# Two more engines in a hand-written order: GpSimd's sums, SyncE's loads and the copy of O^T in a graph-attention kernel

## The chip, the cores and the metric

The kernel runs on one core of a Trainium2 chip. The metric is the device time of one execution in microseconds (us), and lower is better. The kernel before was run three times: 2642.13, 2642.48 and 2645.84 us, so its median is 2642.48 us.

A core has five engines that work side by side, each through its own queue of instructions: TensorE (PE; its weight loads are PEld), VectorE (DVE), ScalarE (ACT), GpSimd (POOL) and SyncE (SP). Here SyncE issues nearly all DMA transfers and computes nothing. An instruction that needs another engine's result waits on a semaphore.

## The reference

There are 128 graphs (blocks) `b` of 128 nodes with 512 features, and a 0/1 adjacency matrix per graph. Two layers follow each other:

```python
# layer 0: attention with 8 heads of 64 features, masked by adj
q, k, v = x @ Wq + bq, x @ Wk + bk, x @ Wv + bv
attn = softmax(where(adj > 0, q k^T / 8, -1e9))        # per head
x = layernorm(x + relu((attn @ v) @ Wo + bo))
# layer 1: graph attention with one head
Wh = x @ W
e = leaky(Wh @ a1 [rows] + Wh @ a2 [columns])          # 128 x 128 per graph
att = softmax(where(adj > 0, e, -9e15), axis=1)        # over the rows
x = layernorm(x + leaky(att @ Wh))
```

## The kernel before

**Products by seven multiplications.** The products with Wq, Wk, Wv, Wo and W are each split into 2 x 2 blocks and done with seven block products in place of eight (`strassen`, a list of seven steps p1, p5, p6, p2, p7, p4, p3). The left operand needs sums of its blocks, which GpSimd makes in `left_blocks` with four additions (L289 to L292): `xS` for x, `oS` for the attention output, `x1S` for the first layer's result. The sums of the weights are made once. Seven weight blocks for Wv [...] lie in DRAM and come back for each group through a ring of three buffers `wv_n` (`fetch`, L402). Each of the seven block products of V first fetches the block that will be wanted two products later.

**Groups, pairs and steps.** Q, K and V are computed for four graphs at a time, a *group*: 3 x 7 = 21 block products (`products`, L361). The products with Wo and W are done for two graphs, a *pair* (`project_o` and `project_w`, both through `pair_product`, L442). One big loop over `t` from -4 to 136 is a software pipeline; one turn is a *step*. In a step, TensorE does the logits of graph `t` (`Softmax`, L486), the attention product of graph `t - 1` (`attend`, L549), five of the group's block products (six where t mod 4 = 3), the seven of a pair (with Wo in odd steps, with W in even steps), and the second layer's small products (`EdgeSoftmax`, `Finish`) for graphs `t - 7` and `t - 8`. The calls `group()` and `pair()` in the loop take the next steps of those lists, so the order of the lines in the loop is a timetable.

**Transposes.** x must be transposed for the products. `load_x` (through `spread`, L257, four DMAs) brings a graph in such a form that VectorE's transpose of 32 x 32 tiles (`transpose_blocks`, L262) completes it. It lands in one of three buffers `xz`. The first layer's result goes the same way: it is normalized (L577), written to DRAM as `x1_dram` (L590), spread back into an `xz` buffer, and transposed into `x1T`. The attention weights `pa` take the same detour: `Softmax.spread` writes `pa_dram` (L528), and when it has landed, reads it as `paz` with four DMAs (L532).

**Normalization.** `norm_stats` takes mean and variance on VectorE and forms `rstd` on GpSimd with two small operations (L571, L573), for which VectorE's `normalize` waits.

**What sets the order.** `tc.manual_schedule(engines=...)` makes the engines that it names keep the order in which the program's lines call them. Before, these are TensorE, VectorE and ScalarE. For GpSimd and SyncE the framework's planner chooses an order by its own costs and priorities, where the data allow it; `norm_stats` asks it for a high priority of the two `rstd` operations. Either way the order is fixed when the kernel is built, and each queue runs in it.

**Around the change.** In the step as written before, a load of x, a residual load (`load_residual`, L273) and a mask load (L465) stand at the start. The last-but-one VectorE lines of a step are `transpose_x(t + 8)`, `mask(t + 1)` and, in even steps, `transpose_x1` for two graphs. The sums `xS` follow the fourth transpose of a group, which lies in the step with t mod 4 = 3. `attend` ends with ScalarE's copy of O^T (L559); in odd steps it begins a new pair and therefore a new use of the only buffer `oT`, which the products with Wo of the pair before read until their last step; in even steps the copy is followed by the sums `oS`. `later` holds work that the next step does right after the logits: the second graph's `store`.

## Time and profile before

| | |
|---|---|
| median of three runs | 2642.48 us |
| the profiled execution's own time | 2641.05 us |
| its span, first to last instruction | 2638.9 us |
| PE busy | 2467.2 us (93%) |
| DVE busy | 1780.2 us (67%) |
| ACT busy | 1355.0 us (51%) |
| POOL busy | 764.3 us (29%) |
| all transfers | 379.89 MB, 144 GB/s |
| mean granted TensorE clock | 0.987 |

The profile is one execution, taken by the hardware profiler. The span is what its records cover; the execution's own time is a little longer. In the timeline, a line gives the start and the duration in us from the span's start, the engine, the line of the kernel, the operation, what it writes and reads, how many instructions were merged, and in brackets how long the engine had been idle before it and what ended that idle time. SPq lines are issues of DMAs, not their transfers; those land later, after the time that the page's table of DMA issues gives. The view of waits lists who waited for whom: the total, how many times, and the longest.

### The profile page before, as it was taken

Reading aid. Unit: us, or ns where it says so; the run is one execution under the profiler, and the core shown is the slowest. Engines: PE = TensorE matmul, PEld = TensorE weight load, DVE = VectorE, ACT = ScalarE, POOL = GpSimd, SP = SyncE. Lnnn points to the kernel's source line nnn. Section 1 sums busy time; section 2 is a strip of 40 time slices with the busy share of each in tenths; the row PEclk is TensorE's granted clock in tenths of the full one; section 3 lists DMA queues with packets and bytes.
Section 4 is the critical chain, followed back from the end, with each engine's and each line's share of the span. In section 5 each row is a group of like instructions: output and inputs, shape, how many; then the busy total and the mean of one; then the engine's idle time right before and its main releaser. Section 6 shows DMA issues by size and latency. Waiting matters only on the chain.

```text
span 2638.9 us, 43141 instructions
## 1 busy us (share of the span) xinstructions
PE 2467.2 (93%) x13717; PEld 1999.8 (76%) x13717; DVE 1780.2 (67%) x3758; ACT 1355.0 (51%) x4801; POOL 764.3 (29%) x1161
## 2 busy tenths in 40 slices
PE   7889999999999999999999999999999999999975
PEld 6767777777777777777777777777777777777753
DVE  4566666676766676766676766676766676766775
ACT  2445455455455555555555555555555555455551
POOL 1122332323332323332323332323332323332222
PEclk9989999999999999999999999999999999999987
DMA  6534454444445444444444445444444444444441
GB/s 186 152 112 133 154 150 148 144 148 143 152 147 153 139 151 143 148 147 156 136 153 143 146 147 156 137 147 144 150 147 155 136 148 144 150 147 152 128 136 49
DMA packets 353348, 379.89 MB, mean 144 GB/s; under 512 B 39640, under 2 KB 257760, under 8 KB 353120
## 3 DMA queue, kind: packets, MB, share of 16 engines
q1 hardware_dynamic: 351824, 376.07, 46.1%
q8 instruction: 109, 1.79, 0.3%
q10 hardware_dynamic: 1296, 1.05, 0.1%
q14 instruction: 119, 0.97, 0.1%
HBM read 240.91 MB, written 136.05 MB: 143 GB/s over the span
## 4 chain that ended last, share of the span: by engine, by line
PE 59%; DVE 15%; ACT 8%; POOL 7%; issue 6%; DMA 3%; SPq 2%; DVEq 0%; ACTq 0%; POOLq 0%
PE st_y L361 14%; PE p_y L442 13%; PE st_w L361 7%; PE st_x L361 6%; PE p_w L442 5%; PE p_oT L549 5%; ACT pa L507 4%; PE lg L486 3%; DVE pa L495 3%; PE p_h L674 2%; PE p_x L442 2%; POOL xS L290 2%; DVE z L683 2%; DVE z L682 2%; DVE xT L262 1%
## 5 line engine op out<-in xcount | busy, mean ns | idle before, releaser
L507 ACT ACTIVATE pa<-pa,nmax 128x128 f32<-128x128 f32 x1024 | 397.7, 391 | 126.6 <-DVE nmax L501 120.5
L521 ACT ACTIVATE pa<-pa,rs 128x128 f32<-128x128 f32 x1024 | 334.3, 397 | 0.6 <-DVE rs L517 0.4
L571 POOL TENSOR_SCALAR ve<-mv 128x1 f32<-128x1 f32 x256 | 62.6, 244 | 934.4 <-DVE mv L568 934.4
L262 DVE STREAM_TRANSPOSE x1T<-xz 128x512 f32<-128x512 f32 x128 | 83.5, 690 | 215.9 <-DMA xz<-x_dram 200.5
L486 PEld LDWEIGHTS lg<-kT,qT 64*128 64x128 f32 x2048 | 124.2, 187 | 93.7 <-issue 93.7
L507 ACT ACTIVATION_READ_ACCUMULATOR pa<-pa,nmax 128x1 f32 x1024 | 193.3, 189 | 0.0
L442 PE MATMUL p_y<-w,x1S 128*128 128x257 f32 x512 | 137.4, 391 | 56.6 <-ACT pr_t L453 56.6
L559 ACT COPY oT<-p_oT 128x512 f32<-128x512 f32 x128 | 74.8, 585 | 214.7 <-PE p_w L442 212.6
L338 ACT COPY st_t<-st_y 128x512 f32<-128x512 f32 x192 | 110.5, 576 | 136.4 <-PE st_y L361 134.0
L453 ACT COPY pr_t<-p_y 128x256 f32<-128x256 f32 (+1 forms) x384 | 139.6, 364 | 77.0 <-PE p_y L442 76.3
L495 DVE TENSOR_TENSOR pa<-lg,mf 128x512 f32<-128x512 f32 x256 | 163.7, 680 | 12.1 <-PE lg L486 8.2
L573 POOL TENSOR_TENSOR rstd<-ve,mhalf 128x1 f32<-128x1 f32 x256 | 166.3, 650 | 18.8
L678 ACT COPY z<-p_h 128x512 f32<-128x512 f32 x128 | 74.9, 585 | 181.7 <-PE p_h L674 181.1
L361 PE MATMUL st_y<-wv_n,xT 128*128 128x256 f32 x512 | 124.4, 386 | 40.9 <-ACT st_t L338 38.5
L536 DVE STREAM_TRANSPOSE paT<-paz 128x1024 f32<-128x1024 f32 x128 | 159.4, 1245 | 4.6 <-DMA paz<-pa_dram 3.9
L342 ACT ACTIVATE st_t<-st_y,b_cols 128x256 f32<-128x256 f32 x192 | 79.8, 467 | 158.3 <-PE st_y L361 158.3
L501 DVE TENSOR_REDUCE nmax<-pa 128x8 f32<-128x1024 f32 x128 | 156.1, 1220 | 4.4
L442 PEld LDWEIGHTS p_y<-w,x1S 128*128 128x128 f32 x512 | 95.3, 192 | 82.3 <-ACT pr_t L453 69.8
L442 PE MATMUL p_y<-wo,oS 128*128 128x256 f32 x512 | 135.9, 388 | 18.1 <-ACT pr_t L453 16.9
L674 PE MATMUL p_h<-wh,att 128*128 128x512 f32 x256 | 133.9, 605 | 18.0 <-DVE att L665 18.0
L289 POOL TENSOR_TENSOR oS<-oT 128x256 f32<-128x256 f32 x64 | 46.5, 726 | 357.0 <-ACT oT L559 357.0
L289 POOL TENSOR_TENSOR xS<-xT 128x512 f32<-128x512 f32 x32 | 40.7, 1273 | 373.0 <-DVE xT L262 357.8
(154 smaller groups left out, 6112.5 us busy)
## 6 DMA issues: line engine op xcount, KB each, us to landing
pa_dram<-pa SPq DMA_DIRECT2D x128, 512.0 KB, 3.0
paz<-pa_dram SPq DMA_DIRECT2D x512, 128.0 KB, 2.9
wv_n<-wv SPq DMA_DIRECT2D x224, 256.0 KB, 2.8
xz<-in_x_dram SPq DMA_DIRECT2D x512, 64.0 KB, 2.2
x<-in_x_dram SPq DMA_DIRECT2D x128, 256.0 KB, 2.8
x_dram<-x SPq DMA_DIRECT2D x128, 256.0 KB, 2.0
xz<-x_dram SPq DMA_DIRECT2D x512, 64.0 KB, 2.2
out_dram<-z SPq DMA_DIRECT2D x128, 256.0 KB, 2.0
```

What stands on the lines that cost most here:

```text
L361: nc.tensor.matmul(p[:, m, :], lhs, rhs, start=start and m == 0 and kc == 0, stop=True, skip_group_check=True,)
L442: nc.tensor.matmul(p[:, :width], xs[n][:, kc, :], w[:, n, kc, :], start=start and kc == 0, stop=True, skip_group_check=True,)
L453: nc.scalar.copy(t[:, :width], p[:, :width])
L486: nc.tensor.matmul(self.lg[r][:, c, :], q[rows, c, cols], k[rows, c, cols], start=True, stop=True)
L495: nc.vector.tensor_add(by_head[:, r * NC : (r + 1) * NC], self.lg[r].rearrange("p c (b k) -> p c b k", b=4), mf.unsqueeze(1).to_broadcast( ...
L501: nc.vector.tensor_reduce(self.nmax, by_head, AX.XY, ALU.max, negate=True)
L507: nc.scalar.activation(self.pa[:, :, h, :], self.pa[:, :, h, :], AF.Exp, bias=self.nmax[:, h : h + 1], accum_out=self.sums[:, h : h + 1],)
L521: nc.scalar.activation(self.pa[:, :, h, :], self.pa[:, :, h, :], AF.Copy, scale=self.rs[:, h : h + 1])
L536: nc.vector.transpose(self.paT.rearrange("p h (a i) -> p a h i", i=32), self.paz.rearrange("p a (h k) -> p a h k", k=32),)
L549: nc.tensor.matmul(p[r * HD : (r + 1) * HD, c, :], v[:, h * HD : (h + 1) * HD], sm.paT[:, r * NC + c, :], start=True, stop=True,)
L573: nc.gpsimd.tensor_tensor(rstd, ve, mhalf, ALU.pow)
L674: nc.tensor.matmul(p.rearrange("p (o f) -> p o f", o=2), edge.att, wh, start=True, stop=True)
```

## The change

SyncE and GpSimd are put under `manual_schedule` too, so that they keep the order of the program's lines. Those lines are moved:

- The transposes of x follow a table `x_turns` by t mod 4: one, two, one and none in place of one per step. The last of a group, and so the sums `xS`, now stands in the step with t mod 4 = 2.
- The loads of x for the next step's transposes stand behind this step's transposes.
- The residual load stands behind `fin.residual()`.
- The first two fetches of Wv's blocks stand at K's first block product instead of its fourth, five block products earlier.
- `attend` returns its copy of O^T (with the sums `oS`) as a function. In even steps it is called at once, in odd steps behind the last two steps of the chain with Wo.
- In `project_o` the first graph's store and the spreads of both graphs are done together at the start of the next step; the second graph's store stays at the end of its chain.
- The exponential of the last head stands behind the output store and one pair product.

```diff
@@ products
-        fetch_first = chains[1][3]
+        fetch_first = chains[1][0]
 ...
-        chains[1][3] = with_fetch
+        chains[1][0] = with_fetch
@@ attend
-        if h == 0:
-            OT[pair] = work.tile([P, NC, 2 * P], F32, name="oT")
-        nc.scalar.copy(OT[pair][:, :, h * P : (h + 1) * P], p)
-        if h == 1:
-            sums = work.tile([P, 3, 2, P], F32, name="oS")
-            OT[pair] = left_blocks(OT[pair], sums)
+
+        def copy():
+            if h == 0:
+                OT[pair] = work.tile([P, NC, 2 * P], F32, name="oT")
+            nc.scalar.copy(OT[pair][:, :, h * P : (h + 1) * P], p)
+            if h == 1:
+                sums = work.tile([P, 3, 2, P], F32, name="oS")
+                OT[pair] = left_blocks(OT[pair], sums)
+
+        return copy
@@ project_o
-        def store(b, stats):
-            normalize(X1[b], stats)
-            d = dram.tile([P, D], F32, name="x1_dram")
-            nc.sync.dma_start(d, X1[b])
-            X[b, 1] = spread(d)
-
-        stats = {}
+        stats, d = {}, {}
+
+        def store(h):
+            b = 2 * pair + h
+            normalize(X1[b], stats[h])
+            d[h] = dram.tile([P, D], F32, name="x1_dram")
+            nc.sync.dma_start(d[h], X1[b])
+
+        def spread_both():
+            store(0)
+            for h in (1, 0):
+                X[2 * pair + h, 1] = spread(d[h])
 ...
-                    store(b + 1, stats[1])
-                    later.append(lambda: store(b, stats[0]))
+                    store(1)
+                    later.append(spread_both)
@@ the loop
-    engines = {mybir.EngineType.PE, mybir.EngineType.DVE, mybir.EngineType.Activation}
+    engines = {
+        mybir.EngineType.PE,
+        mybir.EngineType.DVE,
+        mybir.EngineType.Activation,
+        mybir.EngineType.SP,
+        mybir.EngineType.Pool,
+    }
 ...
+    x_turns = [(8,), (8, 9), (9,), ()]
 ...
-        if on(t + 9):
-            load_x(t + 9)
-        if on(t - 2):
-            load_residual(t - 2)
 ...
         fin.residual()
+        if on(t - 2):
+            load_residual(t - 2)
 ...
-        sm.exp(6, 7)
+        sm.exp(6)
         fin.store()
         pair()
+        sm.exp(7)
 ...
-        if last is not none:
-            attend(last)
+        copy_o = attend(last) if last is not none else none.copy
+        if t % 2 == 0:
+            copy_o()
         sm.spread()
         group()
-        if on(t + 8):
-            transpose_x(t + 8)
+        for b in x_turns[t % GROUP]:
+            if on(t + b):
+                transpose_x(t + b)
+        for b in x_turns[(t + 1) % GROUP]:
+            if on(t + 1 + b):
+                load_x(t + 1 + b)
 ...
         pair(2)
+        if t % 2 == 1:
+            copy_o()
         group(21 if t % GROUP == GROUP - 1 else 1)
```

## The prediction

> **What bounds the kernel now.** Times are in us. I read the page first, then TensorE's waits, then the timeline of one four-step cycle. On the page TensorE is the busy engine:

> ```profile
> span 2638.9 us, 43141 instructions
> ...
> PE 2467.2 (93%) x13717; PEld 1999.8 (76%) x13717; DVE 1780.2 (67%) x3758; ACT 1355.0 (51%) x4801; POOL 764.3 (29%) x1161
> ```

> No other engine is near its limit, so the time moves only with TensorE's idle time, 2638.9 - 2467.2 = 172 us. Its waits (us in total, times, longest) say what is repeated and what happens once:

> ```profile
> PE p_y L442 <- ACT pr_t L453: 75.0, 52, 5.3
> PE st_y L361 <- ACT st_t L338: 38.5, 32, 1.2
> ```

> The first has its long members in the last steps; the second recurs once in each of the 32 groups. Where in the cycle they lie is seen from the starts of the logits (`lg`), the first matmuls of each step:

> ```profile
> 958.78 1.16 PE L486 MATMUL lg<-kT,qT 64*128 64x128 f32 x16
> ...
> 977.08 1.16 PE L486 MATMUL lg<-kT,qT 64*128 64x128 f32 x16
> ...
> 998.79 1.16 PE L486 MATMUL lg<-kT,qT 64*128 64x128 f32 x16
> ...
> 1018.80 1.16 PE L486 MATMUL lg<-kT,qT 64*128 64x128 f32 x16
> ...
> 1037.57 1.16 PE L486 MATMUL lg<-kT,qT 64*128 64x128 f32 x16
> ```

> These start steps with t mod 4 = 2, 3, 0, 1 and again 2. Lengths: 18.30, 21.71, 20.01, 18.77; sum 78.79. Step 2 has no TensorE wait, so 18.30 is the bare length of an even step. An odd step has two bias matmuls more (0.11 + 0.12): 18.53. Step 3 also has a sixth group product (1.73 from its start to the next matmul): 20.26. A cycle without waits is 18.30 + 20.26 + 18.30 + 18.53 = 75.39, so waits cost 3.40: 1.45 in step 3, 1.71 in step 0, 0.24 in step 1. The timeline of step 3 and the beginning of step 0 shows where the first two come from:

> ```profile
> 988.69 0.69 ACT L521 ACTIVATE pa<-pa,rs 128x128 f32<-128x128 f32 x2
> ...
> 989.41 0.32 SPq L528 DMA_DIRECT2D pa_dram<-pa  x1
> ...
> 991.37 0.32 SPq L402 DMA_DIRECT2D wv_n<-wv  x1
> ...
> 993.15 0.58 ACT L559 COPY oT<-p_oT 128x512 f32<-128x512 f32 x1 [3.58 <-PE p_w L442]
> 993.21 2.36 SPq L532 DMA_DIRECT2D paz<-pa_dram  x4
> ...
> 994.28 1.99 PE L361 MATMUL st_y<-wv_n,xT 128*128 128x256 f32 x8 [1.22 <-ACT st_t L338]
> ...
> 995.65 1.27 POOL L289 TENSOR_TENSOR xS<-xT 128x512 f32<-128x512 f32 x1 [10.81 <-DVE xT L262]
> ...
> 996.11 1.89 PE L361 MATMUL st_w<-wv_n,xT 128*128 128x256 f32 x8
> ...
> 1001.79 0.55 DVE L577 TENSOR_SCALAR x<-x,mv,rstd 128x512 f32<-128x512 f32 x1 [2.16 <-POOL rstd L573]
> ```

> ScalarE's copy of O^T holds its queue for 3.58, because the single `oT` buffer is read until the chain with Wo ends. The `st_t` copy behind it is late, and TensorE waits 1.22. VectorE too is set back, and the sums `xS` begin at 995.65, so `rstd` queues behind 5.5 of GpSimd work and VectorE waits 2.16. Its maxima, the exponentials and the `pr_t` copy are late in turn, until the next step's chain shows it:

> ```profile
> 1010.46 1.14 PE L442 MATMUL p_y<-w,x1S 128*128 128x257 f32 x4 [1.44 <-ACT pr_t L453]
> ```

> [...] SP itself waits for `pa_dram` 102 times, 137.4 in all, and nothing passes it. [...] `wv_n` is issued in 0.32 and lands after 2.8. [...] `x<-y,x` (L585) takes 0.69 alone and 1.39 during `xS`.

> **The change part by part.**

> 1. O^T behind the chain. In odd steps the copy comes after the Wo matmuls for which it waited. ScalarE no longer blocks; the 1.45 of step 3 goes. No PSUM bank is held longer, since the copy ended after that chain before.

> 2. Sums in even steps. The last transpose of a group moves from step 3 to step 2, so odd steps have no sums, and both `rstd` of x1 run at once (0.21 + 0.57 after `mv`). VectorE's 2.16 goes. In step 2 GpSimd now runs oS (4 x 0.73), xS (1.27 + 1.26 + 1.72 + 1.26) and x1S (4 x 0.73) in a row: 11.3 from O^T's copy at 13.8 after the step's start, until 25.1, that is 6.8 into step 3, whose z statistics come at 7.5. Hidden, by 0.7; with contention `rstd` may be 1 late, for which ScalarE has 0.7 idle before `pr_t`. Step 1 has two transposes (0.70 more) and VectorE has 1.37 idle there: nothing.

> 3. exp(7) behind `fin.store` and a pair product. ScalarE's pr_t copy is 0.58 (0.39 + 0.19) earlier. With 2, step 0's maxima end near 4 after its start instead of 7.05; the 1.71 goes.

> 4. Loads of x behind the transposes, both x1 spreads after both stores. Before, x1's second spread waited for an x transpose to free one of three `xz` buffers, and VectorE then waited for it (200.5 over the run). Now no load of x holds a buffer that the spreads need. They issue by about 5 into the even step and are needed at 16 or later. The 0.24 of step 1 goes. The x loads, four or eight issues of 0.46, serve the next step's end.

> 5. First two weight fetches (two DMAs) from step 2 to the start of step 1: used in steps 2 and 3, hidden. Mask (one), residual (one, needed about 8 later), and out store keep slack of several us.

> 6. What SP's strict order adds. The seventh weight fetch (`n = 2`) stands in the fourth group product of step 3, directly behind `sm.spread()`. Before, SP issued it at 991.37, ahead of `paz`. Now it comes after: last divide ends 988.69 + 0.69 = 989.38; `pa_dram` issued 989.41; landed 3.0 later (median on the page), 992.4; four `paz` issues, 1.75 (the run of four at 977.19 took 1.77), 994.2; then the fetch, 2.8 if alone, up to 3.3 behind 512 KB of `paz`: 997.0 to 997.5. Its user is the product at 996.11, which without the 1.45 is due at 994.66. TensorE waits 2.3 to 2.8; I take 2.5. Queued behind it are `p_h` and the next logits, so all of it counts. It can't hide earlier: the last divide follows a `pr_t` copy for which the seventh pair product on TensorE is the release. The other fetches stand before the spread.

> Sum per cycle: -3.40 + 2.5 = -0.9; 30 full cycles: -27. In the last steps exp(7) takes some 0.58 off four long waits: -2. The head's four DVE- and DMA-bound steps: 0, between -5 and +5. Against the profiled execution's 2641.05 (span 2638.9, 2.15 around it): 2612; the median shown is 1.4 above that execution: about 2613. Bounds: a fetch wait of 1.8 gives -50, one of 3.3 gives -5.

> **Rivals.**

> A, likeliest: as summed, 2613, own range 2588 to 2637.

> B: the seventh fetch lands in time, because SP can still issue it before `paz`. For it: before, it did. Against it: SP is in the list of ordered engines, and its wait is its own. Time: 2642.5 - 3.40 x 30 - 2 = 2538.

> C, slower: the fetch is later than I think. Place: the same product in step 3. From a wait of 3.40 on, the cycle loses. If `pa_dram` needs 4.0 (from 989.41 it was 3.8 to the first `paz`), `paz` 2.36 as at 993.21, and the fetch 3.3, the data come at 999.1, a wait of 4.4: +1.0 x 30, 2672. Against it: those long figures were made with a weight and a mask transfer among them, which are now elsewhere.

> **How the numbers follow.** A 0.60, B 0.08, C 0.25, and 0.07 that A and C meet near zero. About 0.2% (5.3 us) is what a measurement can tell from no change. Faster is A and B, 0.68; same 0.07; slower 0.25. The range leaves out B and the upper part of C: 2575 to 2670.

> **What would show it.** Right: no 3.58 before the O^T copy, no wait of `x` for `rstd`, x1T not waiting for DMA; steps 0, 1, 2 near 18.3, 18.5, 18.3; step 3 near 22.8 with one wait of 2 to 3 at `st_w<-wv_n,xT` released by DMA `wv_n`. Wrong: that wait absent (B) or over 3.4 (C), or `pr_t` waits left in steps 0 or 1.

## The result, and the profile after

Times are in us. The changed kernel takes 2689.3 (median of 4 runs, 2686.4 to 2692.72) where the kernel before took 2643.95 beside it (4 runs): a ratio of 1.0172, 95% interval 1.0154 to 1.019. It is 1.7% slower; the forecast was 1.1% faster. The profiled execution took 2687.35 with a span of 2685.4, 46.5 more than the span before.

The first part of the page of the changed kernel (busy time of each engine, share of the span, instructions):

```profile
span 2685.4 us, 43419 instructions
PE 2501.6 (93%) x13717; PEld 2033.8 (76%) x13717; DVE 1814.7 (68%) x3758; ACT 1353.9 (50%) x4801; POOL 796.3 (30%) x1161
```

TensorE executes the same 13717 matmuls, and yet it is busy 34.4 longer (2501.6 against 2467.2). A wait counts as idle time, so nearly all of this is matmuls that became longer. Its idle time, 183.8, is only 12 above the 172 of before. TensorE's waits in the changed kernel (us in total, times, longest):

```profile
PE st_w L361 <- DMA wv_n<-wv: 103.6, 31, 4.6
PE p_y L442 <- ACT pr_t L453: 25.9, 13, 5.0
```

The `st_t` wait (38.5) has gone and the `pr_t` wait fell from 75.0 to 25.9. In their place stands one new wait, for the seventh weight fetch, once in each of 31 cycles, 3.34 on average. The starts of the logits in the timeline of one cycle show where it lies:

```profile
1064.37 1.16 PE L486 MATMUL lg<-kT,qT 64*128 64x128 f32 x16
...
1082.68 1.16 PE L486 MATMUL lg<-kT,qT 64*128 64x128 f32 x16
...
1109.33 1.16 PE L486 MATMUL lg<-kT,qT 64*128 64x128 f32 x16
...
1127.63 1.16 PE L486 MATMUL lg<-kT,qT 64*128 64x128 f32 x16
```

Step 2 lasts 18.31, step 3 26.65, step 0 18.30, and step 1 (up to 1146.12) 18.49. Three of four steps have reached their bare length; step 3 alone, against a bare 20.26, spoils the cycle. The timeline of the second half of that step, SP's queue (SPq) and TensorE:

```profile
1094.86 0.70 ACT L521 ACTIVATE pa<-pa,rs 128x128 f32<-128x128 f32 x2
...
1095.58 0.32 SPq L528 DMA_DIRECT2D pa_dram<-pa  x1
...
1098.83 1.79 SPq L532 DMA_DIRECT2D paz<-pa_dram  x4
...
1100.72 0.38 SPq L402 DMA_DIRECT2D wv_n<-wv  x1
...
1103.97 3.75 PE L361 MATMUL st_w<-wv_n,xT 128*128 128x256 f32 x8 [3.59 <-DMA wv_n<-wv]
...
1107.52 1.88 PE L683 MATMUL p_h<-wh,att 128*128 128x512 f32 x2
```

This is the order that part 6 of the prediction described: `pa_dram`, a wait for its landing, four `paz`, then the fetch. But after the wait the eight matmuls of `st_w` take 3.75, where the same eight took 1.89 before, and `p_h` takes 1.88 instead of 1.02. The view of these stretches says why (stretch, its length, PE busy and matmuls, PEld, DVE, ACT, POOL busy, granted TensorE clock, DMA share, GB/s):

```profile
1082.70:1100.40 17.70, 17.68 (x105) 14.84 (x104) 13.50 (x27) 9.61 (x35) 8.48 (x11) 1.00 0.40 129
1100.40:1104.00 3.60, 0.03 (x1) 0.06 (x1) 1.63 (x4) 0.58 (x1) 1.73 (x3) 0.78 0.89 245
1104.00:1107.50 3.50, 3.50 (x8) 2.80 (x9) 0.00 (x0) 0.00 (x0) 0.00 (x0) 0.50 0.31 104
1107.50:1109.30 1.80, 1.80 (x3) 0.34 (x1) 1.15 (x2) 0.00 (x0) 0.00 (x0) 0.52 0.00 0
1109.30:1127.60 18.30, 18.30 (x105) 15.12 (x104) 11.42 (x24) 11.10 (x40) 4.55 (x8) 1.00 0.35 114
```

The granted clock falls from 1.00 to half during the wait, stays there over the next 5.3 us of work, and is full again in the next step. So the wait is paid twice: 3.59 idle, and 5.3 of work at half speed, which loses another 2.8 (26.65 - 20.26 - 3.59). In the whole run the mean clock is 0.966, before it was 0.987.

The step lasts 25.34 on average over 31 cycles: 20.26 bare, 3.34 of wait, and 1.74 that is neither. Without the first cycle, whose bare step is shorter, and against 20.22, the bare length in the runs below, this last loss is 1.86. It isn't spread evenly: 0.24 in 8 cycles, 1.66 to 1.93 in 8, 2.67 to 2.88 in 14. In the 8 cycles the recorded clock stays at 1.00 throughout, so 0.24 comes with the wait itself and 1.62 is the clock's share.

The other thing to see is at the start of step 3. The timeline there, GpSimd (POOL) beside VectorE and ScalarE:

```profile
1086.33 1.23 DVE L691 SCALAR_TENSOR_TENSOR z<-z 128x512 f32<-128x512 f32 x1
...
1087.09 1.05 POOL L290 TENSOR_TENSOR x1S<-x1S,x1T 128x256 f32<-128x256 f32 x1
...
1087.59 1.10 DVE L692 TENSOR_TENSOR z<-z,x 128x512 f32<-128x512 f32 x1
...
1088.62 0.81 DVE L661 SCALAR_TENSOR_TENSOR e<-e 128x128 f32<-128x128 f32 x1
...
1090.18 0.40 ACT L669 ACTIVATE att<-att,nmax 128x128 f32<-128x128 f32 x1 [1.26 <-DVE nmax L665]
```

The same three VectorE instructions in step 3 of the kernel before, where GpSimd's sums had ended at 980.08:

```profile
980.74 0.68 DVE L682 SCALAR_TENSOR_TENSOR z<-z 128x512 f32<-128x512 f32 x1
...
981.45 0.69 DVE L683 TENSOR_TENSOR z<-z,x 128x512 f32<-128x512 f32 x1
...
982.06 0.28 DVE L652 SCALAR_TENSOR_TENSOR e<-e 128x128 f32<-128x128 f32 x1
```

The sums `xS` and `x1S` now end 7.4 into step 3 (6.8 forecast). While they run, VectorE's three instructions take 3.14; before, they took 0.68 + 0.69 + 0.28 = 1.65. ScalarE then waits 1.26 for VectorE (before, it did not wait there), its divides are later, and `pa_dram` is issued 12.91 after the step's start (median), where it was 12.33.

### The profile page after: what moved, and what is told of

The parts are those of the page before. It is cut to its first block, busy times and chain, and to the rows that moved or that the text cites. A ratio compares the mean times of both kernels' runs of the same rounds, so it can differ in the third digit from the quotient of the medians.

```text
span 2685.4 us, 43419 instructions
## 1 busy us (share of the span) xinstructions
PE 2501.6 (93%) x13717; PEld 2033.8 (76%) x13717; DVE 1814.7 (68%) x3758; ACT 1353.9 (50%) x4801; POOL 796.3 (30%) x1161
## 3 DMA queue, kind: packets, MB, share of 16 engines
q8 instruction: 109, 1.79, 0.3%
q10 hardware_dynamic: 1296, 1.05, 0.1%
## 4 chain that ended last, share of the span: by engine, by line
PE 85%; DMA 6%; DVE 4%; ACT 3%; issue 1%; SPq 1%; POOL 0%; DVEq 0%; POOLq 0%; ACTq 0%
PE st_y L361 23%; PE p_y L442 15%; PE st_w L361 14%; PE p_w L442 7%; PE st_x L361 6%; PE lg L486 5%; PE p_h L683 5%; PE p_oT L549 4%; DMA wv_n<-wv 4%; PE p_x L442 4%; DMA pa_dram<-pa 1%; ACT pa L507 1%; ACT pa L521 1%; DVE z L691 1%; DVE z L692 1%
## 5 line engine op out<-in xcount | busy, mean ns | idle before, releaser
L575 POOL TENSOR_SCALAR ve<-mv 128x1 f32<-128x1 f32 x256 | 68.4, 267 | 1362.7 <-DVE mv L572 1362.7
L521 ACT ACTIVATE pa<-pa,rs 128x128 f32<-128x128 f32 x1024 | 332.9, 395 | 0.1
L486 PEld LDWEIGHTS lg<-kT,qT 64*128 64x128 f32 x2048 | 126.3, 190 | 105.9 <-issue 105.9
L338 ACT COPY st_t<-st_y 128x512 f32<-128x512 f32 x192 | 110.2, 574 | 175.9 <-PE st_y L361 175.9
L361 PE MATMUL st_w<-wv_n,xT 128*128 128x256 f32 x256 | 97.3, 547 | 103.6 <-DMA wv_n<-wv 103.6
L379 DVE TENSOR_TENSOR v<-st_w,st_t 128x512 f32<-128x512 f32 x64 | 44.2, 691 | 206.4 <-PE st_w L361 150.1
L577 POOL TENSOR_TENSOR rstd<-ve,mhalf 128x1 f32<-128x1 f32 x256 | 176.0, 688 | 21.3
L453 ACT COPY pr_t<-p_y 128x256 f32<-128x256 f32 (+1 forms) x384 | 140.3, 365 | 77.1 <-PE p_y L442 76.4
L683 PE MATMUL p_h<-wh,att 128*128 128x512 f32 x256 | 148.8, 666 | 18.0 <-DVE att L674 18.0
L289 POOL TENSOR_TENSOR oS<-oT 128x256 f32<-128x256 f32 x64 | 46.3, 724 | 398.1 <-ACT oT L561 398.1
L361 PEld LDWEIGHTS st_w<-wv_n,xT 128*128 128x128 f32 x256 | 67.2, 275 | 127.6 <-issue 106.7
L486 PE MATMUL lg<-kT,qT 64*128 64x128 f32 x2048 | 150.8, 287 | 0.0
L549 PEld LDWEIGHTS p_oT<-paT,v 128*64 128x64 f32 x2048 | 111.2, 138 | 46.0 <-issue 32.9
L442 PE MATMUL p_y<-w,x1S 128*128 128x257 f32 x512 | 133.2, 382 | 13.4 <-ACT pr_t L453 13.4
```

The source lines that it names most:

```text
L361: nc.tensor.matmul(p[:, m, :], lhs, rhs, start=start and m == 0 and kc == 0, stop=True, skip_group_check=True,)
L442: nc.tensor.matmul(p[:, :width], xs[n][:, kc, :], w[:, n, kc, :], start=start and kc == 0, stop=True, skip_group_check=True,)
L453: nc.scalar.copy(t[:, :width], p[:, :width])
L486: nc.tensor.matmul(self.lg[r][:, c, :], q[rows, c, cols], k[rows, c, cols], start=True, stop=True)
L521: nc.scalar.activation(self.pa[:, :, h, :], self.pa[:, :, h, :], AF.Copy, scale=self.rs[:, h : h + 1])
L549: nc.tensor.matmul(p[r * HD : (r + 1) * HD, c, :], v[:, h * HD : (h + 1) * HD], sm.paT[:, r * NC + c, :], start=True, stop=True,)
```

## The experiments

Two theories at first. **F**: the whole loss is the seventh fetch standing behind the spread, by its wait and by the clock that the wait lowers; without it all steps are bare and the kernel is far faster than before. **G**: other parts of the change cost as well (the sums that end late, SP's and GpSimd's strict order), and the fetch only shows it.

**The fetch ahead of the spread.** The changed kernel with the fourth group product, which issues the fetch, one place earlier; nothing else is touched:

```diff
-        sm.spread()
         group()
+        sm.spread()
```

> The changed kernel with one pair of lines exchanged: the fourth group product of a step, with its fetch of a block of Wv, stands ahead of the spread of the attention weights. Theory 1, the late seventh fetch and the clock that falls after the wait for it: both go in all 31 cycles, 31 x (3.34 + 1.74) = 157 us, so about 2532 us, step 3 near 20.3 us, granted clock back at 0.987. Theory 2, GpSimd's three sums in a row in step 2 are what costs: the wait reappears elsewhere in step 3 and the time stays above 2640 us.

Measured: 2528.06 (2 runs), ratio to the kernel before 0.9556 (0.9529 to 0.9584). Its page, and the first line of TensorE's waits, where the fetch is no longer among them:

```profile
span 2525.3 us, 43417 instructions
PE 2446.0 (97%) x13717; PEld 2009.7 (80%) x13717; DVE 1817.4 (72%) x3758; ACT 1355.6 (54%) x4801; POOL 797.1 (32%) x1161
```

```profile
PE p_y L442 <- ACT pr_t L453: 25.3, 11, 5.0
```

The end of its step 3 in the timeline of TensorE, and SP's queue there:

```profile
1024.92 1.89 PE L361 MATMUL st_y<-wv_n,xT 128*128 128x256 f32 x8
1026.64 1.89 PE L361 MATMUL st_w<-wv_n,xT 128*128 128x256 f32 x8
1028.37 1.02 PE L683 MATMUL p_h<-wh,att 128*128 128x512 f32 x2
1029.32 0.94 PE L486 MATMUL lg<-kT,qT 64*128 64x128 f32 x12
```

```profile
1019.60 0.89 SPq L402 DMA_DIRECT2D wv_n<-wv  x2
1022.03 0.32 SPq L528 DMA_DIRECT2D pa_dram<-pa  x1
1024.64 3.01 SPq L532 DMA_DIRECT2D paz<-pa_dram  x4
```

The fetch is now issued before SP starts to wait for the divides; `st_w` follows `st_y` with no gap and at full speed, and the steps last 18.30, 20.22, 18.31 and 18.49. `pa_dram` is issued just as late as in the changed kernel (12.93 after the step's start), and here that costs nothing. Theory F holds: once the fetch is ahead, nothing that G names costs time. (What it costs where the fetch is late, the last pair of runs shows.) The difference to the changed kernel splits by two lines of the pages: TensorE idle 183.8 - 79.3 = 104.5, which is 31 waits of 3.37, and TensorE busy 2501.6 - 2446.0 = 55.6, which is 31 times 1.79 for the same matmuls. Of this 1.79, 0.24 comes with the wait itself, as seen above, and the rest with the lower clock.

**SP left to the planner.** The changed kernel with only GpSimd added to the ordered engines:

```diff
         mybir.EngineType.Activation,
-        mybir.EngineType.SP,
         mybir.EngineType.Pool,
```

> The changed kernel with SyncE taken out of the list of engines that keep the program's order; GpSimd stays in it. Theory 1, SyncE's strict order is what makes the seventh fetch late: the planner puts that fetch ahead of the reads of the attention weights, as in the kernel before, and the wait and the lower clock go: about 2535 to 2560 us, the upper end if the planner's order brings back VectorE's wait for x1. Theory 2, GpSimd's order costs: above 2640 us.

Measured: 2527.1 (2 runs), ratio 0.9553 (0.9523 to 0.9582), steps as in the run above. The planner issues the fetch before `paz`. So all that the change loses comes from fixing SP's order with the spread ahead of the fetch; every other edit can stay.

**TensorE kept at work during the wait.** If the lower clock is a cost of its own, matmuls whose result nobody reads, placed where TensorE would otherwise wait, should make the kernel faster. First ten of them, before the product that waits:

```diff
-        group(21 if t % GROUP == GROUP - 1 else 1)
+        group()
+        if t % GROUP == GROUP - 1 and group_steps:
+            p = psum("p_fill")
+            for _ in range(10):
+                nc.tensor.matmul(p[:, :HALF], ident, wq[:, 0, 0, :], start=True, stop=True)
+            group(20)
```

> The changed kernel with ten extra matmuls of 128x256 (about 0.216 us each at full clock, 2.2 us in all, their result is not used) ahead of the last two group products of step 3, in front of the wait for the seventh fetch. Theory 1, TensorE's idle time itself lowers the clock: the wait shrinks from 3.3 to about 1.2 us and the clock stays up; the fill is free since it lies inside the wait, so only the clock's share goes, 31 x 1.74 = 54 us: about 2635 us at a clock near 0.987. Theory 3, the lower clock has another cause than the idle time: the clock stays at 0.966 and the time near 2689 us.

Measured: 2668.44 (3 runs), ratio 1.0087 (1.0062 to 1.0112), clock 0.986. The expectation missed because I had sized the ten at 2.16; they took 4.32 per cycle (each call is two matmuls in the trace), longer than the wait itself, of which 1.0 in the whole run was left. Even so the kernel is 21 faster than the changed one, although TensorE has 138 more to do. The run was repeated with half of them:

```diff
-            for _ in range(10):
+            for _ in range(5):
```

> The changed kernel with five extra matmuls (2.16 us per cycle; ten took 4.32 us) in front of the wait for the seventh fetch, their result not used. The wait of the changed kernel was 3.34 us per cycle in the mean and the time lost to the lower clock 1.74 us. Theory 1, idle time lowers the clock and the wait is set by the fetch alone: the fetch comes at the same time, so step 3 keeps 20.22 + 3.3 us but loses the clock's 1.7 us, 31 x 1.7 = 53 us less: about 2636 us, with a wait of 1.2 us left and a clock near 0.987. Theory 3, the clock is independent of the wait: no change, 2689 us.

Measured: 2648.05 (10 runs), ratio 1.0007 (0.9998 to 1.0016), 41 less than the changed kernel; clock 0.985. The wait, TensorE's timeline, and the two stretches of one step 3 (columns as above):

```profile
PE st_w L361 <- DMA wv_n<-wv: 39.7, 31, 2.7
```

```profile
1070.76 1.89 PE L361 MATMUL st_y<-wv_n,xT 128*128 128x256 f32 x8
1072.49 2.32 PE L826 MATMUL p_fill<-wq,ident 128*128 128x256 f32 x10
1076.24 1.97 PE L361 MATMUL st_w<-wv_n,xT 128*128 128x256 f32 x8 [1.43 <-DMA wv_n<-wv]
1078.04 1.02 PE L683 MATMUL p_h<-wh,att 128*128 128x512 f32 x2
```

```profile
1055.00:1070.00 15.00, 15.00 (x94) 12.82 (x94) 10.95 (x21) 9.03 (x34) 7.94 (x9) 1.00 0.40 134
1070.00:1079.00 9.00, 7.58 (x35) 5.72 (x33) 4.96 (x12) 1.17 (x2) 2.27 (x4) 1.00 0.57 156
```

The fetch comes no earlier: 2.16 of extra matmuls and 1.28 of mean wait are 3.44, where the changed kernel waits 3.34. But the clock stays at 1.00 in this step, where the changed kernel fell to half, and the eight matmuls after the wait take 1.97 in place of 3.75; over the run the mean clock is 0.985, as in the runs with the fetch ahead (0.985 to 0.987). Of 1.74 per cycle 41 / 31 = 1.33 came back, less than the 1.7 expected: part of the rest is the 0.24 that a wait brought at full clock in the 8 cycles above, and the lines show where it lies. Back to back, a product starts 0.17 before the modelled end of the one before it (in the first run, 1026.64 against 1024.92 + 1.89), and a wait takes this overlap away; and the product after the wait takes 1.97 instead of 1.89. The expectation had counted this 0.24 as the clock's. That the clock is a cost of its own is shown; by this run it is worth at least 41.

**The copy of O^T alone.** The kernel before, with only the copy moved behind the chain with Wo in odd steps:

```diff
+        def copy():
             ...
+        return copy
...
-        if last is not none:
-            attend(last)
+        copy_o = attend(last) if last is not none else none.copy
+        if t % 2 == 0:
+            copy_o()
...
         pair(2)
+        if t % 2 == 1:
+            copy_o()
```

> The kernel before with one part of the change alone: in odd steps the copy of O^T stands behind the chain with Wo. By the prediction's first part the wait for st_t in step 3 goes, 31 x 1.45 = 45 us: about 2599 us. If the copy's stall also was what made VectorE and so the sums and rstd late (second part), the wait of step 0 shrinks too, by up to 29 x 1.71 = 50 us: down to 2549 us. If the sums are late by themselves, step 0 keeps its 1.71 us.

Measured: 2591.36 (2 runs), ratio 0.9796 (0.9767 to 0.9824), between the two expectations. Step 3 lasts 20.22, so its 1.45 is gone as predicted. Step 0 fell as well, from 20.02 to 19.23, and step 1 rose from 18.87 to 19.43 (medians). TensorE's wait that is left, in steps 0 and 1:

```profile
PE p_y L442 <- ACT pr_t L453: 64.3, 63, 5.3
```

The copy brings 1.49 + 0.79 - 0.56 = 1.72 per cycle, 53 over 31 cycles, as measured. Of step 0's 1.71 it takes nearly half; that the blocked ScalarE had set back VectorE there too is likely, but only argued.

**The sums of x one block per step, twice.** What the new timetable of the sums is worth depends on whether something waits for SP in step 3. So I put it back to one block per step, first with the fetch ahead of the spread, then in the changed kernel as it is:

```diff
-    x_turns = [(8,), (8, 9), (9,), ()]
+    x_turns = [(8,), (8,), (8,), (8,)]
```

> The version with the fetch ahead of the spread, and the x transposes back at one per step, so that the sums of x are made in step 3 again. By the prediction's second part the sums stand in front of the two rstd of x1 there, VectorE waits for them and step 0 loses up to 1.7 us: 29 x 0.9 to 1.7 = 26 to 49 us more than 2528 us, 2554 to 2577 us. If the place of the sums is worth nothing once the copy of O^T is out of the way: 2528 us.

> The changed kernel with the x transposes back at one per step; the late fetch stays. In the changed kernel the sums in step 2 run on into step 3 beside VectorE's work on z, and the write of the attention weights there is issued 12.9 us after the step's start, 12.3 before. If the sums make it late: issued at 12.3 again, the fetch 0.6 us earlier, step 3 shorter by 0.6 us of wait and up to 1.7 us of clock, and step 0 hardly longer since TensorE's wait gives VectorE time: 31 x 0.6 to 2.3 = 19 to 71 us less, 2618 to 2670 us. If the sums have no part in it: 12.9 stays and the time is 2689 us or more.

Measured with the fetch ahead: 2558.99 (2 runs), ratio 0.9668 (0.965 to 0.9686), 31 more than with the new timetable. Nearly all of it lies in step 0 (19.22 instead of 18.31). VectorE's waits in this kernel have again the one that part 2 was to remove:

```profile
DVE x L581 <- POOL rstd L577: 97.5, 63, 2.4
```

Measured with the fetch left behind: 2654.42 (5 runs), ratio 1.0015 (0.9996 to 1.0033), 35 less than the changed kernel. `pa_dram` is issued at 12.33 again, and the wait has shrunk:

```profile
PE st_w L361 <- DMA wv_n<-wv: 75.6, 28, 4.5
```

Three more of these waits are listed under other releasers; the page has 83.5 of idle time before this product, 2.69 per cycle, against 103.6. TensorE is also busy 14.0 less (2487.6). VectorE's three instructions take 0.68, 0.69 and 0.28 again in the timeline of the run with the fetch ahead (1029.63 to 1031.24).

So the new timetable of the sums gains 31 in one setting and loses 35 in the other. The sums beside VectorE in step 3 make `pa_dram` 0.58 late (12.91 against 12.33); it matters only when TensorE waits for what SP issues next.

**The best version again.** The fetch ahead of the spread, in more runs:

> The version with the fetch ahead of the spread once more, in five rounds, for the interval: 2528 us, 4.4% below the kernel before.

Measured: 2527.38 (5 runs, 2525.47 to 2529.66) beside 2646.23 (20 runs) of the kernel before: ratio 0.9549 (0.9536 to 0.9563), 4.5% faster than before and 6% faster than the changed kernel.

## Why the prediction was wrong

The wait that was named was the right one, and the gain was about right; the cost was too small by more than half, because the wait was longer and because a second cost that follows from it was not in the sum. In spans:

| Term | predicted | measured | how |
|---|---|---|---|
| waits removed | -3.40 x 30 - 2 = -104 | -113.6 | fetch-ahead run against before, 2525.3 - 2638.9 |
| wait for the seventh fetch | +2.5 x 30 = +75 | +104.5 | idle time, changed kernel against fetch-ahead run |
| longer matmuls after that wait: about 48 by the clock, 7 (31 x 0.24) by the wait itself | not in the sum | +55.6 | busy time of the same two |
| sum | -29 | +46.5 | |

**Parts 1, 2 and 3** removed what they were said to remove: steps 0, 1 and 2 last 18.31, 18.49 and 18.30 where 18.30, 18.53 and 18.30 were forecast. The attribution was off. I gave step 0's 1.71 to the sums and exp(7); the copy alone takes 0.79 of it, and the sums the other 0.92 (the run with one block per step has 19.22). In step 0 nothing is then left for exp(7). Step 1 is another matter: it lasts 19.43 with the copy alone, and its bare 18.49 in the run with one block per step and the fetch ahead. Something in parts 3 to 5 or in the fixed order brings that; which of them was not tested.

**Part 2's side effect** was the first wrong step. I wrote that the sums in step 3 are "Hidden, by 0.7; with contention `rstd` may be 1 late, for which ScalarE has 0.7 idle". The 0.7 was misread: in the step 3 of before that the prediction shows, the statistics of z end 6.79 after the step's start, not 7.5. And I looked only at GpSimd's own result, `rstd`, which is not held up by the sums, as the statistics now end at 8.28. The contention works the other way: GpSimd's sums slow three VectorE instructions from 1.65 to 3.14, and over ScalarE's divides that puts off `pa_dram`. I had just this in front of me, `x<-y,x` at 0.69 alone and 1.39 during `xS`, and then costed it in the wrong direction.

**Parts 4 and 5** came out as nothing, as costed: no wait of TensorE for loads of x or for the first two fetches, and `x1T` no longer waits for a DMA.

**Part 6** is the step that failed. The order in SP's queue was right to the instruction, the sizes were not. Against the chain as I added it up, by medians: `pa_dram` 0.58 late (shown above to come from the sums); from its issue to the first `paz` 2.66 (mean 2.80), 3.0 forecast; from `paz` to the fetch 1.84, 1.75 forecast; from the fetch to the product 3.34 (mean 3.56, up to 4.5), where I took 2.8, the page's median before, to 3.3, an estimate of mine. The product is due about 0.1 later than I wrote. Each miss is small, but the wait is the rest of a subtraction: by the medians it would be 3.05, and the longer fetches bring its mean to 3.34, where 2.5 was forecast. My range for it, 1.8 to 3.3, ended just below.

Larger is the term that I didn't have. "TensorE waits 2.3 to 2.8 [...] so all of it counts" takes a wait to cost its length, and "the time moves only with TensorE's idle time", at the prediction's start, takes its busy time as fixed. The trace of the changed kernel shows otherwise: the granted clock is 0.50 after the wait and 1.00 a step later, and the 22 half-clock spells away from the kernel's head and tail (190 to 2533 after the start) are recorded at 3.41 (8 of them) or twice that (14). Half of 3.41 is 1.7 and half of 6.83 is 3.4. The 8 cycles that lost 1.66 to 1.93 have half-clock time of 3.41 each, the 14 that lost 2.67 to 2.88 have 6.83; less the 0.24, these losses fit one spell spent at work, fully or nearly so, and two partly spent in the wait. The length of a single wait does not tell the cycles apart: some waits from 2.52 on already brought the loss, while one of 3.49 brought none.

**The rivals.** Rival C had the right place, and its time, 2672, was nearest. But its deciding point, "From a wait of 3.40 on, the cycle loses", was wrong for the same reason: the mean wait was 3.34, just below, and the cycle lost 1.65 (18.31 + 18.49 + 18.30 + 25.34 = 80.44, mean of 31 cycles, against 78.79). The changed kernel with one block per step shows that break-even lies lower: with a mean wait of 2.69 and a mean clock of 0.970 it took as long as the kernel before (1.0015). So at the 2.5 that I forecast the change would have gained little, by this estimate. Rival B is what the fetch-ahead version does: 2538 forecast, 2527 measured. The range ended at 2670 because A and C were spread over the wait alone; a loss that some waits brought (1.66 to 2.88) and others of nearly the same length did not has no place in such a range.

## What to carry to other kernels

A wait on TensorE isn't priced by its length alone: a wait of 2.5 to 4.5 that recurs in every cycle cost half as much again in clock (31 waits of 3.34, and about 48 in all by the clock), while at the marks in the changed kernel's trace before which TensorE had been idle for 1.90 or less of the last 3.41 the clock stayed. So look at the granted clock in the stretch after a wait, and treat a forecast that removes several short waits and leaves one long one with suspicion. In a DMA queue that keeps a written order put everything that doesn't depend on the wait ahead of the instruction that waits: here a fetch of 256 KB stood behind a round trip through DRAM, and exchanging two lines turned 1.7% slower into 4.5% faster. Where two engines contend, ask which of the two is on the path.

## What was not expected of the hardware

- Matmuls that nobody reads can pay. Filling 2.16 of a wait of 3.4 with them raised the mean clock from 0.966 to 0.985 and made the kernel 41 faster, although TensorE had 69 more to do and the fetch came no earlier.
- VectorE lost more beside GpSimd's sums than I had assumed: 0.68 became 1.23, 0.69 became 1.10, and a 128x128 instruction of 0.28 became 0.81. GpSimd's own sum of 0.73 became 1.05 to 1.17.
- The weight fetch, 2.8 from issue to landing on the page before, took 3.34 (up to 4.5) from issue to the product that waits for it, directly behind the four `paz` on the same queue and ahead of four loads of x; the DMA engines were busy 0.89 of that stretch.
